# A ConvNeXt block on one core: the first product in pairs of triples, with three PSUM accumulators each

## The chip, the cores and the metric

The kernel runs on one core of a Trainium2 chip. The metric is the device time of one execution, in microseconds; smaller is better. A core has TensorE (PE, its weight loads are PEld), VectorE (DVE), ScalarE (ACT), GpSimd (POOL), and SyncE (SP), which here only issues DMAs.[...] Matmuls write to PSUM[...]; ScalarE and VectorE read it from there[...].

## The reference

A ConvNeXt block is followed by a gate. The input has 32 images of 384 channels and 28 x 28 pixels (784), all in fp32.

```python
# layer 0
y = depthwise_conv7x7(x) + dw_b                  # 384 channels
y = layernorm over channels (ln_g, ln_b)
y = y @ w1 + b1                                  # 384 -> 1536
y = gelu(y)                                      # the exact one
gx = sqrt(sum over pixels of y*y)                # per image and feature
nx = gx / (mean over features of gx + 1e-6)
y = grn_g * (y * nx) + grn_b + y
y = y @ w2 + b2                                  # 1536 -> 384
x = x + y
# layer 1: a gate for each image and channel
avg, mx, mn = mean, max, min of x over the pixels
logits = concat(avg @ W1.T, grouped(mx, W2_1) * W2_2, mn @ W3.T) @ Wfc.T
x = sigmoid(logits[:, :, None, None] + x)
```

## The kernel before

The kernel has two parts. In the first, up to about 496 us, the depthwise convolution of all images is made as matmuls with banded matrices and written to DRAM. GpSimd also makes combined weights there (form_w, L268) and SP stores them to u1d and u2d, one store a step.

The second part goes image by image. For each image, up makes the first product (L559) and down the second (L651). Up of image b+1 stands before down of image b (the loop at L824). Both products use a bilinear scheme: a product of blocks 3 x 3 by 3 x 2 is made with 15 matmuls in place of 18, at the price of additions. The six operand blocks are named 0a to 2b (a and b are the two halves of the pixels), and sums of blocks have the names p to z. They are the "forms": forms_up (L520) makes them for the first product from the normalised image, nine in tiles of their own, and forms (L624) makes them for the second product, each with 128 x 1568 elements.

In up there are KT = 4 triples of three feature blocks each. A triple runs the 15 steps of UPSTEPS (L91). A step has an operand, the weights' sum, a PSUM bank by letter, whether the bank is started anew (1) or added to (0), and what is read from the bank afterwards. "copy" is a copy by ScalarE (L583); "add", "sub", "rsub", "plus" and "minus" are reads by VectorE that combine the bank with what stands in the result y or in a spare tile E (L585 to L593). The banks' values are read in the middle of a sum: bank A, for one, is copied after step x, added to in step v, read again, and so on. A matmul that adds to a bank therefore has to wait until the last reader of that bank is done. A triple uses six banks, A, B, C, D, H and F; D, H and F serve one step each (z, t and 2b). The pool of banks (psz, L416) has seven, in turn for up, down and the transposes of turn. The weights of a triple come in one load of 960 KB, in two buffers (up1, L407).

The result y of a triple then goes through gelu (L549), and square (L553) sums its squares for grn (L602), both on ScalarE. grn makes a scale for each feature. scale (L620) applies it to all 12 blocks of y, on ScalarE for most images, and only then can GpSimd make the forms of the second product. In steady state gelu and square of the triples t-1 and t-2 stand within up; the last gelus, six squares, grn and the scalings stand in the hooks of the down that follows (beside, L735). The same down carries turn (L486) and forms_up for the image after: turn normalises, transposes on TensorE, and ScalarE moves the result out of PSUM.

The program's order is not the order that the engines get. A list scheduler places each instruction by its own estimate of when it can run; so in before it puts the steps z, t and 2b of the first triple of an image ahead of v (banks D, H and F in the trace stand right after A, B and C). In each engine's queue that order is fixed.

Images 0 and 1 start with hooks of their own (start_hooks, L779), since there is no second product yet that could hide their statistics (stats, L458) and transposes.

Of the kernel before, what the change touches and what calls it, by code (L numbers as in the profile page):

```python
# [13 lines left out]
P = 128  # L14
C = 384
# [74 lines left out]

UPSTEPS = (  # L91
# [8 lines left out]
    ("z", "-12", "D", 1, (("D", "add", "2b"),)),  # L100
    ("0b", "-10+11", "A", 0, (("A", "copy", "1b"), ("D", "rsub", "1b"))),
    ("0a", "-00", "B", 0, (("B", "sub", "0a"),)),
    ("t", "+00+10-11", "H", 1, (("H", "add", "E"),)),
    ("q", "-00+01+02-10+11", "A", 0, (("A", "plus", "0b"),)),
    ("u", "+00+10+12", "B", 0, (("B", "minus", "1a"),)),
    ("2b", "-12-20+21+22", "F", 1, (("F", "add", "2b"),)),
)
KT = FB // 3

# [10 lines left out]
def convnext_gate_kernel(  # L120
# [34 lines left out]
    dww = const.tile([P, CB, 49], F32, name="dww")  # L155
    nc.sync.dma_start(dww, dw_w.rearrange("(cb p) t -> p cb t", p=P))
# [8 lines left out]
    awt = const.tile([P, 2, CB, R], F32, name="awt")  # L165
    w22b = const.tile([P, R], F32, name="w22b")
# [8 lines left out]
    with ExitStack() as one:  # L175
# [8 lines left out]
        ws = tp.tile([P, CB * FF], F32, name="ws")  # L184
        tab = tp.tile([P, CB, FL], F32, name="tab")
        dwb = tp.tile([P, C], F32, name="dwb")

# [78 lines left out]
        U1, U2 = 4, 22  # L266

        def form_w(name, wv, text, dst):  # L268

            t = ufp.tile([P, KT, P], F32, tag="uf", name=name)  # L270
            for n, (sg, m, k) in enumerate(terms(text)):
                blk = wv[:, :, int(k), m, :]
                if n == 0:
                    nc.gpsimd.tensor_scalar(t, blk, float(sg), None, ALU.mult)
                else:
                    nc.gpsimd.tensor_tensor(t, t, blk, ALU.add if sg > 0 else ALU.subtract)
            nc.sync.dma_start(dst, t)
# [37 lines left out]
        for s in range(NK):  # L315
# [80 lines left out]
            if si == SK - 1:  # L396
                xt = xn
            i = s - U1
# [8 lines left out]
    up1 = ctx.enter_context(tc.tile_pool(name="up1", bufs=2))  # L407
    up2 = ctx.enter_context(tc.tile_pool(name="up2", bufs=6))
    tep = ctx.enter_context(tc.tile_pool(name="tep", bufs=2))
# [8 lines left out]
    def bank(name):  # L418
        return psz.tile([P, 512], F32, tag="pz", name=name)

    gate = const.tile([P, 3, CB, 3 * R], F32, name="gate")
    nc.vector.memset(gate, 0.0)
    nc.vector.tensor_scalar(gate[:, 0, :, 0:R], awt[:, 0], 1.0 / NT, None, ALU.mult)
    nc.vector.tensor_copy(gate[:, 2, :, 2 * R : 3 * R], awt[:, 1])
    grp = const.tile([P, CB, R], F32, name="grp")
    for cb in range(CB):
        nc.vector.tensor_scalar(grp[:, cb, :], w22b, w21_t[:, cb : cb + 1], None, ALU.mult)

    G = C // R
    grp_a = const.tile([P, CB, R], F32, name="grp_a")
    nc.gpsimd.affine_select(
        out=grp_a, in_=grp, pattern=[[P, CB], [-G, R]], compare_op=ALU.is_ge,
        fill=0.0, base=0, channel_multiplier=1,
    )
    grp_b = const.tile([P, CB, R], F32, name="grp_b")
    nc.gpsimd.affine_select(
        out=grp_b, in_=grp_a, pattern=[[-P, CB], [G, R]], compare_op=ALU.is_ge,
        fill=0.0, base=G - 1, channel_multiplier=-1,  # L440
    )
    nc.vector.tensor_copy(gate[:, 1, :, R : 2 * R], grp_b)
# [102 lines left out]
    def run(hooks, key):  # L545
        for fn in hooks.get(key, ()):
            fn()
# [11 lines left out]
    def up(b, hooks, squares=True):  # L559

        o = feats.pop(b)
        ym = ys[b] = yp.tile([P, FB, NT], F32, tag="y", name=f"y_{b}")
        for t in range(KT):
            wt = up1.tile([P, NS, P], F32, tag="u1", name=f"u1_{b}_{t}")
            nc.sync.dma_start(wt, u1d[t])
            banks = {}
            z = {
                f"{m}{'ab'[h]}": ym[:, 3 * t + m, h * NH : (h + 1) * NH]
                for m in range(3)
                for h in range(2)  # L570
            }
            z["E"] = tep.tile([P, NH], F32, tag="te", name=f"te_{b}_{t}")
            for i, (opnd, _, bk, first, acts) in enumerate(UPSTEPS):
                if first:
                    banks[bk] = bank(f"ph_{b}_{t}_{bk}")
                nc.tensor.matmul(  # L576
                    banks[bk][:, :NH], wt[:, i, :], o[opnd],
                    start=(first == 1), stop=True, skip_group_check=True,
                )
                for src, how, to in acts:  # L580
                    p, d = banks[src][:, :NH], z[to]
                    if how == "copy":
                        nc.scalar.activation(d, p, AF.Identity)  # L583
                    elif how == "add":
                        nc.vector.tensor_tensor(d, d, p, ALU.add)  # L585
                    elif how == "sub":
                        nc.vector.tensor_tensor(d, d, p, ALU.subtract)  # L587
                    elif how == "rsub":
                        nc.vector.tensor_tensor(d, p, d, ALU.subtract)
                    elif how == "plus":  # L590
                        nc.vector.tensor_tensor(d, p, z["E"], ALU.add)  # L591
                    else:
                        nc.vector.tensor_tensor(d, p, z["E"], ALU.subtract)  # L593
                if i in (3, 7, 11):
                    m = (i - 3) // 4
                    if t >= 1:
                        gelu(b, 3 * (t - 1) + m)
                    if t >= 2 and squares:
                        square(b, 3 * (t - 2) + m)
                run(hooks, (t, i))  # L600
# [134 lines left out]
    def beside(b):  # L735
        hooks = {}

        def at(step, fn, *args):
            hooks.setdefault(step, []).append(lambda: fn(*args))

        n = b + 1
        last = n == B - 1
        if n < B:
            for m in range(3):
                at(0, gelu, n, FB - 3 + m)
        if b + 2 < B:
            for j in range(NJ):
                at((0, 0, 1, 1, 2, 2, 3)[j], turn, b + 2, j)
            at(3, forms_up, b + 2)
        if b + 3 < B:  # L750
            at(3, load_y, b + 3)
        if n < B:
            f0 = 0 if b == 0 else FB - 6
            for i in range(f0, FB):
                at((i - f0) // 3 if last else 4 + (i - f0) // (2 if b else 4), square, n, i)
        if b + 3 < B:
            at(8, stats, b + 3)
            at(8, std, b + 3)
        if n < B:
            at(2 if last else 8, grn, n)  # L760
        if b >= 1 and not last:
            at(9, gate_store, b - 1)
        if n < B:
            at(9 if b else 0, load_x, n)
        if n < B:
            for f in range(FB):
                at((2 if last else 10) + f // 3, scale, n, f)
            if last:
                at(6, forms, n, 0, 4)
                at(9, forms, n, 4, EARLY)  # L770
            else:
                at(NS - 1, forms, n, 0, EARLY)
        if b >= 1 and last:
            at(7, gate_store, b - 1)
        return hooks

    def start_hooks():  # L779
        h0, h1 = {}, {}  # L780

        def at(h, t, i, fn, *args):
            h.setdefault((t, i), []).append(lambda: fn(*args))

        V, A = nc.vector, nc.scalar
        if B > 1:
            at(h0, 0, 8, stats, 1)
            at(h0, 0, 8, std, 1)
            for j in range(NJ):
                at(h0, 1, 1 + 2 * j, turn, 1, j, V)  # L790
            at(h0, 1, NS - 1, forms_up, 1)
        if B > 2:
            at(h0, 2, 6, load_y, 2)
        for m in range(3):
            at(h1, 0, 1 + 2 * m, gelu, 0, FB - 3 + m)
        for i in range(6):
            at(h1, i // 5, (8, 10, 11, 12, 13, 0)[i], square, 0, FB - 6 + i)
        if B > 2:
            at(h1, 0, 5, stats, 2)
        at(h1, 1, 1, grn, 0)  # L800
        if B > 2:
            at(h1, 1, 1, std, 2)
        for f in range(FB):
            at(h1, 1 + (6 + f) // 12, (6 + f) % 12, scale, 0, f, A if f % 2 else V)
        at(h1, 2, 8, forms, 0, 0, EARLY)
        return h0, h1

    h0, h1 = start_hooks()
    stats(0)
    std(0)  # L810
    for j in range(NJ):
        turn(0, j, (nc.scalar, nc.vector)[j % 2], (nc.scalar, nc.vector, nc.scalar))
    forms_up(0, nc.vector)
    if B > 1:
        load_y(1)
    up(0, h0)
    load_x(0)
    if B > 1:
        up(1, h1, squares=False)
    else:  # L820
        for fs in h1.values():
            for fn in fs:
                fn()
    for b in range(B):  # L824
        if b >= 1 and b + 1 < B:
            up(b + 1, {})
        down(b, beside(b))
# [40 lines left out]
```

## Time and profile before

| | us |
|---|---|
| median of three runs (3218.94 to 3219.2) | 3219.02 |
| the profiled execution, its time | 3216.78 |
| the profiled execution, its span | 3215.1 |
| depthwise part, to the last matmul of it | about 496 |
| first product, image 10 | 40.33 |
| second product, image 9, with its transposes | 43.86 |

| ScalarE, one instruction | mean ns | count |
|---|---|---|
| scale, 784 columns (L484) | 1027 | 378 |
| gelu (L551) | 941 | 384 |
| square (L557), and its accumulator read | 851 and 189 | 384 each |
| copy of a bank in up (L583) | 483 to 496 | 640 |
| table load | 1283 | 97 |

VectorE's reads of a bank in up take 558 to 567 ns, a form of the second product on GpSimd 3512 to 3518, one of the first 1020.

How to read it: the times of the page are sums over the profiled execution. A row of a group has the busy time, the mean of one instruction, and the idle time of the engine just before, with what ended it. In the rows of the order in time, the columns are start and length in us, the engine and line, the operation, and how many instructions stand in the row. One fp32 matmul appears as two passes, each with its weight load, and a pass of 392 columns lasts longer (492 ns) than the distance to the next (329 ns), since they are pipelined.

### The profile page before, as it was taken

To read this page: it belongs to the slowest core of one execution; us is meant where nothing else is said; L and a number is where in the kernel's file an instruction comes from. 1 tells how busy PE (TensorE), PEld (TensorE's weight loads), DVE (VectorE), ACT (ScalarE), POOL (GpSimd) and SP (SyncE) were. 2 spreads that over 40 slices of the span, in tenths; PEclk is the share of its full clock that TensorE was granted. 3 is DMA by queue.
4 is the path that set the end of the run, shared out by engine and by line. 5 is a ranking of instruction groups with operands and counts; after the bars stand their busy time and mean duration, and the time that the engine had idled before them with its cause. 6 is when DMAs were issued, how large, how long until landed. Compare 5 with 4: busy or idle time off the path is not lost.

```text
span 3215.1 us, 35678 instructions
## 1 busy us (share of the span) xinstructions
PE 3174.8 (99%) x12352; PEld 2009.1 (62%) x12352; DVE 1669.3 (52%) x3442; ACT 1886.1 (59%) x3032; POOL 1607.1 (50%) x821
## 2 busy tenths in 40 slices
PE   8999998999999999999999999999999999999998
PEld 7999995555555555555555555555555555555555
DVE  3443436555555555555555555555555555555553
ACT  2222225766666666666666666666666666666662
POOL 2453511645555555555555555555555555555554
PEclk9999999999999999999999999999999999999999
DMA  9999985444444444344444444444444444444333
GB/s 346 364 340 359 341 296 183 131 131 136 130 139 143 141 141 139 132 136 143 134 142 145 134 145 143 136 140 139 146 146 129 137 129 141 142 141 141 125 101 126
DMA packets 257160, 540.84 MB, mean 168 GB/s; under 512 B 121021, under 2 KB 130774, under 8 KB 247766
## 3 DMA queue, kind: packets, MB, share of 16 engines
q1 hardware_dynamic: 244148, 500.70, 46.1%
q10 hardware_dynamic: 12834, 37.88, 3.5%
q8 instruction: 98, 1.61, 0.2%
q14 instruction: 80, 0.66, 0.1%
HBM read 447.53 MB, written 90.99 MB: 167 GB/s over the span
## 4 chain that ended last, share of the span: by engine, by line
PE 98%; DVE 1%; ACT 1%; DMA 1%; issue 0%; SPq 0%; ACTq 0%; POOL 0%; DVEq 0%; POOLq 0%
PE ph_A L576 14%; PE ph_B L576 13%; PE pz_A L673 11%; PE pz_B L673 10%; PE pz_C L673 5%; PE pz_E L673 5%; PE ph_C L576 5%; PE pc L344 5%; PE pc L345 4%; PE pc L348 4%; PE pz_F L673 3%; PE ph_D L576 3%; PE ph_H L576 3%; PE ph_F L576 3%; PE pz_G L673 3%; PE pz_D L673 3%
## 5 line engine op out<-in xcount | busy, mean ns | idle before, releaser
L648 POOL TENSOR_TENSOR d_v<-d_u,y 128x1568 f32<-128x1568 f32 x32 | 112.4, 3512 | 759.4 <-PE pz_B L673 735.4
L551 ACT ACTIVATE y<-y,fv 128x784 f32<-128x784 f32 x384 | 346.7, 941 | 214.5 <-DVE y L591 213.8
L484 ACT ACTIVATE y<-y,fv,gsc 128x784 f32<-128x784 f32 x378 | 358.6, 1027 | 30.1 <-DVE gsc L618 30.1
L557 ACT ACTIVATE junk<-y 128x784 f32<-128x784 f32 x384 | 326.7, 851 | 5.0
L648 POOL TENSOR_TENSOR d_p<-y 128x1568 f32<-128x1568 f32 x31 | 109.1, 3518 | 434.7 <-ACT y L484 434.7
L576 PE MATMUL ph_A<-af,u 128*128 128x392 f32 x768 | 313.7, 502 | 5.5 <-DVE af L542 5.4
L362 ACT ACTIVATE yc<-pc,dwb 128x224 f32<-128x224 f32 x192 | 103.8, 641 | 367.1 <-PE pc L348 264.4
L576 PE MATMUL ph_B<-af,u 128*128 128x392 f32 x768 | 311.3, 493 | 0.3 <-ACT y L583 0.3
L673 PE MATMUL pz_A<-y,u 128*128 128x392 f32 x768 | 268.8, 493 | 0.0
L648 POOL TENSOR_TENSOR y<-d_v,y 128x1568 f32<-128x1568 f32 x64 | 223.4, 3514 | 2.5
L576 PEld LDWEIGHTS ph_A<-af,u 128*128 128x128 f32 x768 | 136.4, 190 | 135.3 <-ACT y L583 57.8
L576 PE MATMUL ph_A<-acc,u 128*128 128x392 f32 x512 | 216.4, 504 | 0.0
L344 PE MATMUL pc<-xt,tmat 128*128 128x224 f32 x768 | 209.4, 354 | 6.7 <-issue 4.9
L576 PE MATMUL ph_B<-acc,u 128*128 128x392 f32 x512 | 213.6, 499 | 0.1
L576 PEld LDWEIGHTS ph_B<-af,u 128*128 128x128 f32 x768 | 145.2, 190 | 109.0 <-DVE y L587 9.6
L673 PEld LDWEIGHTS pz_A<-y,u 128*128 128x128 f32 x768 | 145.8, 190 | 106.4
L583 ACT ACTIVATE y<-ph_A 128x392 f32<-128x392 f32 x256 | 124.7, 487 | 145.0 <-PE ph_A L576 144.9
L237 POOL COPY xpad<-xi 128x784 f32<-128x784 f32 x96 | 80.6, 841 | 254.4 <-PE pt L248 188.1
L587 DVE TENSOR_TENSOR y<-y,ph_A 128x392 f32<-128x392 f32 x128 | 72.0, 563 | 238.9 <-PE ph_A L576 228.1
L473 ACT ACTIVATE sd<-mv,eps_t 128x7 f32<-128x7 f32 x32 | 9.6, 300 | 314.3 <-DVE mv L468 314.3
L542 POOL TENSOR_TENSOR af<-af,acc 128x392 f32<-128x392 f32 x186 | 187.2, 1020 | 4.9
L348 PE MATMUL pc<-xt,tmat 128*128 128x192 f32 x768 | 187.6, 326 | 0.0
(160 smaller groups left out, 7007.1 us busy)
## 6 DMA issues: line engine op xcount, KB each, us to landing
u<-u1d SPq DMA_DIRECT2D x128, 960.0 KB, 4.7
u<-u2d SPq DMA_DIRECT2D x480, 256.0 KB, 2.7
tmat<-fs SPq DMA_DIRECT2D x48, 1420.0 KB, 9.3
yd<-yc SPq DMA_DIRECT2D x22, 1792.0 KB, 8.4
yi<-yd SPq DMA_DIRECT2D x32, 1232.0 KB, 6.8
xi<-in_x SPq DMA_DIRECT2D x96, 392.0 KB, 9.4
x<-in_x SPq DMA_DIRECT2D x32, 1176.0 KB, 5.8
out<-x ACTq DMA_DIRECT2D x31, 1176.0 KB, 5.0
```

What stands on the lines that cost most here:

```text
L344: nc.tensor.matmul(pc[:, ci, :N], t[:, c, P : 2 * P], xc, start=True, stop=False)
L345: nc.tensor.matmul(pc[:REACH, ci, : N - B], t[:, c, 2 * P : T0 + MW], xc[:, B:], start=False, stop=False)
L348: nc.tensor.matmul(pc[:, ci, B:N], t[:, c, :P], xc[:, : N - B], start=False, stop=True)
L362: nc.scalar.activation(yc[:, :, :, cy + ci].rearrange("p b j -> p j b"), pc[:, ci, :N].rearrange("p (j b) -> p j b", j=NJ), AF.Identity, b ...
L484: eng.activation(out, in_, AF.Identity, bias=add, scale=mul)
L542: eng.tensor_tensor(d, o[in0], o[in1], op)
L551: nc.scalar.activation(y, y, AF.Gelu, bias=b1_t[:, f : f + 1], scale=1.0)
L557: nc.scalar.activation(junk, ys[b][:, f, :], AF.Square, accum_out=ssqs[b][:, f : f + 1])
L576: nc.tensor.matmul(banks[bk][:, :NH], wt[:, i, :], o[opnd], start=(first == 1), stop=True, skip_group_check=True,)
L583: nc.scalar.activation(d, p, AF.Identity)
L648: nc.gpsimd.tensor_tensor(d, o[in0], o[in1], op)
L673: nc.tensor.matmul(pz[:, :NH], wt[:, t, :], o[opnd][:, t, :], start=(first == 1 and t == 0), stop=(t == KT - 1), skip_group_check=True,)
```

## The change

The first product takes two triples together: each step is done for triple t2 and then for t2+1. Each triple has only the banks A, B and C; z, t and 2b start C anew. Weights come in thirds of five steps, in six buffers of the size of a third. Gelu and square leave the loop of up. Their places are given by hooks for each image (within, beside): in the steady state six gelus and three squares in the second pair of up, the others in down, and the 12 scalings of the image before in the first pair of up, with the blocks that the form p reads put first. grn is one step later. Image 1 starts in another way too.

```diff
-    ("z", "-12", "D", 1, (("D", "add", "2b"),)),
-    ("0b", "-10+11", "A", 0, (("A", "copy", "1b"), ("D", "rsub", "1b"))),
+    ("z", "-12", "C", 1, (("C", "add", "2b"),)),
+    ("0b", "-10+11", "A", 0, (("A", "copy", "1b"), ("C", "rsub", "1b"))),
...
-    ("t", "+00+10-11", "H", 1, (("H", "add", "E"),)),
+    ("t", "+00+10-11", "C", 1, (("C", "add", "E"),)),
...
-    ("2b", "-12-20+21+22", "F", 1, (("F", "add", "2b"),)),
+    ("2b", "-12-20+21+22", "C", 1, (("C", "add", "2b"),)),
...
+UG = 5
...
-    up1 = ctx.enter_context(tc.tile_pool(name="up1", bufs=2))
+    up1 = ctx.enter_context(tc.tile_pool(name="up1", bufs=6))
...
-    tep = ctx.enter_context(tc.tile_pool(name="tep", bufs=2))
+    tep = ctx.enter_context(tc.tile_pool(name="tep", bufs=3))
...
-        for t in range(KT):
-            wt = up1.tile([P, NS, P], F32, tag="u1", name=f"u1_{b}_{t}")
-            nc.sync.dma_start(wt, u1d[t])
...
-                if i in (3, 7, 11):
-                    m = (i - 3) // 4
-                    if t >= 1:
-                        gelu(b, 3 * (t - 1) + m)
-                    if t >= 2 and squares:
-                        square(b, 3 * (t - 2) + m)
-                run(hooks, (t, i))
+        for t2 in range(0, KT, 2):
             for i, (opnd, _, bk, first, acts) in enumerate(UPSTEPS):
+                for t in (t2, t2 + 1):
+                    if i % UG == 0:
+                        wts[t] = up1.tile([P, UG, P], F32, tag="u1", name=f"u1_{b}_{t}_{i}")
+                        nc.sync.dma_start(wts[t], u1d[t, :, i : i + UG, :])
...
+                    if first and i < 3:
+                        banks[t, bk] = bank(f"ph_{b}_{t}_{bk}")
...
+                    run(hooks, (t2, 2 * i + t - t2))
```

The hooks of up in the new kernel (V is VectorE, A is ScalarE, HF = 6; a key is the pair's first triple and the matmul in the pair):

```python
order = [f for f in range(FB) if f % 3] + [f for f in range(FB) if f % 3 == 0]

def squared(b):
    return 0 if b == 1 else HF if b in (0, B - 1) else HF // 2

def within(b):
    hooks, at = adder()
    p = b - 1
    if b == 0:
        if B > 1:
            at((0, 12), stats, 1)
            at((0, 12), std, 1)
            for j in range(NJ):
                at((0, 18 + 2 * (j // 2)), turn, 1, j, V)
            at((0, 24), forms_up, 1)
...
    elif b == 1:
        for m in range(HF):
            at((0, 2 + 2 * m), gelu, p, HF + m)
            at((0, 16 + 2 * m), square, p, HF + m)
...
        at((0, 29), grn, p)
...
        for i, f in enumerate(order):
            at((2, 1 + i), scale, p, f, V if i % 3 else A)
        at((2, 12), forms, p, 0, EARLY)
    else:
        for i, f in enumerate(order):
            at((0, 2 * i), scale, p, f)
        at((0, 24), forms, p, 0, EARLY)
    if b != 1:
        for m in range(HF):
            at((2, 2 + 4 * m), gelu, b, m)
        for m in range(squared(b)):
            at((2, 28 if m >= HF // 2 else 22 + 2 * m), square, b, m)
    return hooks
```

In beside, the remaining gelus stand in steps 0 and 1 of the second product, the remaining squares from step 3 on (step 1 for the last image), grn in step 9 (4), gate_store in step 10 (9). The scalings stand there only for the last image.

Three smaller edits go with it. form_w no longer issues its store; a list holds it, and it is issued at the next step of the depthwise part. The gate's weights are made in a function called at step 40 of that part in place of after it, and the second affine_select writes to gate directly. The tiles dww, awt, w22b, grp and grp_a are in the pool that is released after the depthwise part.

More of the change, by code (lines that the diff above doesn't have):

```diff
@@ L152, in convnext_gate_kernel @@
     yl = dram.tile([P, NLAST, B, NJ * YC], F32, name="yl")
-    dww = const.tile([P, CB, 49], F32, name="dww")
-    nc.sync.dma_start(dww, dw_w.rearrange("(cb p) t -> p cb t", p=P))
     ident = const.tile([P, P], F32, name="ident")
@@ L164, in convnext_gate_kernel @@
     nc.gpsimd.memset(ones_f, 1.0 / FF)
-    awt = const.tile([P, 2, CB, R], F32, name="awt")
-    w22b = const.tile([P, R], F32, name="w22b")
+    gate = const.tile([P, 3, CB, 3 * R], F32, name="gate")
     wfc = const.tile([3 * R, C], F32, name="wfc")
@@ L184, in convnext_gate_kernel @@
         ws = tp.tile([P, CB * FF], F32, name="ws")
+        dww = tp.tile([P, CB, 49], F32, name="dww")
+        nc.sync.dma_start(dww, dw_w.rearrange("(cb p) t -> p cb t", p=P))
         tab = tp.tile([P, CB, FL], F32, name="tab")
         dwb = tp.tile([P, C], F32, name="dwb")
+        awt = tp.tile([P, 2, CB, R], F32, name="awt")
+        w22b = tp.tile([P, R], F32, name="w22b")
+        grp = tp.tile([P, CB, R], F32, name="grp")
+        grp_a = tp.tile([P, CB, R], F32, name="grp_a")
         NT2 = 4
@@ L266, in convnext_gate_kernel, with gate_weights @@
         U1, U2 = 4, 22
+        stores = []
+        SG = 40
+        def gate_weights():
+            nc.vector.memset(gate, 0.0)
+            nc.vector.tensor_scalar(gate[:, 0, :, 0:R], awt[:, 0], 1.0 / NT, None, ALU.mult)
+            nc.vector.tensor_copy(gate[:, 2, :, 2 * R : 3 * R], awt[:, 1])
+            for cb in range(CB):
+                nc.vector.tensor_scalar(
+                    grp[:, cb, :], w22b, w21_t[:, cb : cb + 1], None, ALU.mult
+                )
+            G = C // R
+            nc.gpsimd.affine_select(
+                out=grp_a, in_=grp, pattern=[[P, CB], [-G, R]], compare_op=ALU.is_ge,
+                fill=0.0, base=0, channel_multiplier=1,
+            )
+            nc.gpsimd.affine_select(
+                out=gate[:, 1, :, R : 2 * R], in_=grp_a, pattern=[[-P, CB], [G, R]],
+                compare_op=ALU.is_ge, fill=0.0, base=G - 1, channel_multiplier=-1,
+            )
         def form_w(name, wv, text, dst):
@@ L276, in form_w @@
                     nc.gpsimd.tensor_tensor(t, t, blk, ALU.add if sg > 0 else ALU.subtract)
-            nc.sync.dma_start(dst, t)
+            stores.append((dst, t))
         AHEAD = 6
@@ L397, in convnext_gate_kernel @@
                 xt = xn
+            if s == SG:
+                gate_weights()
+            for dst, u in stores:
+                nc.sync.dma_start(dst, u)
+            stores.clear()
             i = s - U1
@@ L419, in bank @@
         return psz.tile([P, 512], F32, tag="pz", name=name)
[L423 to L442, printed above, removed]
     x_tiles, yts, sts, accs, pts, feats = {}, {}, {}, {}, {}, {}
@@ L557, in square, with up @@
         nc.scalar.activation(junk, ys[b][:, f, :], AF.Square, accum_out=ssqs[b][:, f : f + 1])
-    def up(b, hooks, squares=True):
+    def up(b, hooks):
         o = feats.pop(b)
         ym = ys[b] = yp.tile([P, FB, NT], F32, tag="y", name=f"y_{b}")
-        for t in range(KT):
-            wt = up1.tile([P, NS, P], F32, tag="u1", name=f"u1_{b}_{t}")
-            nc.sync.dma_start(wt, u1d[t])
[L566 to L572, printed above, removed]
-            for i, (opnd, _, bk, first, acts) in enumerate(UPSTEPS):
[L574 to L593, printed above, removed]
-                if i in (3, 7, 11):
-                    m = (i - 3) // 4
-                    if t >= 1:
-                        gelu(b, 3 * (t - 1) + m)
-                    if t >= 2 and squares:
-                        square(b, 3 * (t - 2) + m)
-                run(hooks, (t, i))
@@ new lines, in up @@
+        wts, banks, zs = {}, {}, {}
+        for t2 in range(0, KT, 2):
+            for i, (opnd, _, bk, first, acts) in enumerate(UPSTEPS):
+                for t in (t2, t2 + 1):
+                    if i % UG == 0:
+                        wts[t] = up1.tile([P, UG, P], F32, tag="u1", name=f"u1_{b}_{t}_{i}")
+                        nc.sync.dma_start(wts[t], u1d[t, :, i : i + UG, :])
+                    if i == 0:
+                        zs[t] = {
+                            f"{m}{'ab'[h]}": ym[:, 3 * t + m, h * NH : (h + 1) * NH]
+                            for m in range(3)
+                            for h in range(2)
+                        }
+                        zs[t]["E"] = tep.tile([P, NH], F32, tag="te", name=f"te_{b}_{t}")
+                    z = zs[t]
+                    if first and i < 3:
+                        banks[t, bk] = bank(f"ph_{b}_{t}_{bk}")
+                    nc.tensor.matmul(
+                        banks[t, bk][:, :NH], wts[t][:, i % UG, :], o[opnd],
+                        start=(first == 1), stop=True, skip_group_check=True,
+                    )
+                    for src, how, to in acts:
+                        p, d = banks[t, src][:, :NH], z[to]
+                        if how == "copy":
+                            nc.scalar.activation(d, p, AF.Identity)
+                        elif how == "add":
+                            nc.vector.tensor_tensor(d, d, p, ALU.add)
+                        elif how == "sub":
+                            nc.vector.tensor_tensor(d, d, p, ALU.subtract)
+                        elif how == "rsub":
+                            nc.vector.tensor_tensor(d, p, d, ALU.subtract)
+                        elif how == "plus":
+                            nc.vector.tensor_tensor(d, p, z["E"], ALU.add)
+                        else:
+                            nc.vector.tensor_tensor(d, p, z["E"], ALU.subtract)
+                    run(hooks, (t2, 2 * i + t - t2))
@@ L729, in gate_store, with adder @@
             nc.scalar.dma_start(ov, xt)
-    def beside(b):
+    HF = FB // 2
+    V, A = nc.vector, nc.scalar
+    order = [f for f in range(FB) if f % 3] + [f for f in range(FB) if f % 3 == 0]
+    def adder():
         hooks = {}
@@ L739, in at, with beside @@
             hooks.setdefault(step, []).append(lambda: fn(*args))
+        return hooks, at
+    def squared(b):
[3 more added lines that the diff above has]
+        p = b - 1
+        if b == 0:
+            if B > 1:
+                at((0, 12), stats, 1)
+                at((0, 12), std, 1)
+                for j in range(NJ):
+                    at((0, 18 + 2 * (j // 2)), turn, 1, j, V)
+                at((0, 24), forms_up, 1)
+            if B > 2:
+                at((2, 0), load_y, 2)
+        elif b == 1:
+            for m in range(HF):
+                at((0, 2 + 2 * m), gelu, p, HF + m)
+                at((0, 16 + 2 * m), square, p, HF + m)
+            if B > 2:
+                at((0, 8), stats, 2)
+            at((0, 29), grn, p)
+            if B > 2:
+                at((0, 29), std, 2)
+            for i, f in enumerate(order):
+                at((2, 1 + i), scale, p, f, V if i % 3 else A)
+            at((2, 12), forms, p, 0, EARLY)
+        else:
+            for i, f in enumerate(order):
[6 more added lines that the diff above has]
+                at((2, 28 if m >= HF // 2 else 22 + 2 * m), square, b, m)
+        return hooks
+    def beside(b):
+        hooks, at = adder()
         n = b + 1
         last = n == B - 1
-        if n < B:
-            for m in range(3):
-                at(0, gelu, n, FB - 3 + m)
         if b + 2 < B:
@@ L752, in beside @@
         if n < B:
-            f0 = 0 if b == 0 else FB - 6
-            for i in range(f0, FB):
-                at((i - f0) // 3 if last else 4 + (i - f0) // (2 if b else 4), square, n, i)
+            g0 = 0 if n == 1 else HF
+            for f in range(g0, FB):
+                at((f - g0) // 3, gelu, n, f)
+            s0 = squared(n)
+            for f in range(s0, FB):
+                at((1 if last else 3) + (f - s0) // 2, square, n, f)
         if b + 3 < B:
             at(8, stats, b + 3)
-            at(8, std, b + 3)
+            at(9, std, b + 3)
@@ L759, in beside @@
         if n < B:
-            at(2 if last else 8, grn, n)
+            at(4 if last else 9, grn, n)
         if b >= 1 and not last:
-            at(9, gate_store, b - 1)
+            at(10, gate_store, b - 1)
         if n < B:
[L764 to L772, printed above, removed]
@@ L773, in beside @@
-        if b >= 1 and last:
-            at(7, gate_store, b - 1)
-        return hooks
[L779 to L806, printed above, removed]
@@ L808, in convnext_gate_kernel @@
-    h0, h1 = start_hooks()
+            at(10 if b else 0, load_x, n)
+        if last:
+            for i, f in enumerate(order):
+                at(4 + i // 3, scale, n, f)
+            at(8, forms, n, 0, 4)
+            at(9, forms, n, 4, EARLY)
+            if b >= 1:
+                at(9, gate_store, b - 1)
+        return hooks
     stats(0)
@@ L811, in convnext_gate_kernel @@
     for j in range(NJ):
-        turn(0, j, (nc.scalar, nc.vector)[j % 2], (nc.scalar, nc.vector, nc.scalar))
-    forms_up(0, nc.vector)
+        turn(0, j, (A, V)[j % 2], (A, V, A))
+    forms_up(0, V)
     if B > 1:
         load_y(1)
-    up(0, h0)
+    up(0, within(0))
     load_x(0)
     if B > 1:
[L819 to L823, printed above, removed]
+        up(1, within(1))
     for b in range(B):
         if b >= 1 and b + 1 < B:
-            up(b + 1, {})
+            up(b + 1, within(b + 1))
         down(b, beside(b))
```

## The prediction

> **What bounds the kernel now.** I read the page's busy times and chain first, then the groups by form, what the weight loads waited for, and the order in time of one image.
>
> ```profile
> PE 3174.8 (99%) x12352; PEld 2009.1 (62%) x12352; DVE 1669.3 (52%) x3442; ACT 1886.1 (59%) x3032; POOL 1607.1 (50%) x821
> ...
> PE 98%; DVE 1%; ACT 1%; DMA 1%; issue 0%; SPq 0%; ACTq 0%; POOL 0%; DVEq 0%; POOLq 0%
> ```
>
> TensorE is busy throughout and is 98% of the chain; every other engine is idle 40% or more. No work of TensorE's is removed, so only the little time in which it issues below its pace can be won. The groups by form show where that is: one matmul is two passes (two records), and a pass of 392 columns that is not held up lasts 492 or 493 ns.
>
> ```profile
> L576 PE MATMUL ph_A<-af,u 128*128 128x392 f32 x768 | 313.7, 502 | 5.5 <-DVE af L542 5.4
> L576 PE MATMUL ph_B<-acc,u 128*128 128x392 f32 x512 | 213.6, 499 | 0.1
> L673 PE MATMUL pz_A<-y,u 128*128 128x392 f32 x768 | 268.8, 493 | 0.0
> ```
>
> The first product (L576) has groups above it, most of the second (L673) has not. What its weight loads waited for, from 545 us on:
>
> ```profile
> PEld ph_A L576 <- ACT y L583: 56.3, 122, 0.8
> PEld ph_A L576 <- ACT te L583: 49.3, 118, 0.6
> PEld ph_B L576 <- DVE te L589: 25.7, 89, 0.4
> PEld ph_B L576 <- DVE y L587: 24.6, 62, 0.8
> ```
>
> An accumulator that is added to again waits until ScalarE has copied, or VectorE has read, its last value. These waits come to 155.9 us, but a weight load stands one pass (0.33 us) ahead of its matmul, so most of that is cover. What reaches the matmuls is read from the order in time, image 10 of 32 here (rows of PE, PEld and ACT from three such answers):
>
> ```profile
> 1143.83 0.82 PE L576 MATMUL ph_A<-af,u 128*128 128x392 f32 x2
> 1144.49 0.82 PE L576 MATMUL ph_B<-af,u 128*128 128x392 f32 x2
> ...
> 1164.02 0.82 PE L576 MATMUL ph_A<-af,u 128*128 128x392 f32 x2
> ...
> 1173.90 0.82 PE L576 MATMUL ph_A<-af,u 128*128 128x392 f32 x2
> ...
> 1184.16 2.80 PE L673 MATMUL pz_G<-y,u 128*128 128x392 f32 x8
> ```
> ```profile
> 1151.08 0.30 PEld L576 LDWEIGHTS ph_B<-acc,u 128*128 128x128 f32 x2 [0.48 <-DVE y L587]
> 1151.82 0.30 PEld L576 LDWEIGHTS ph_A<-acc,u 128*128 128x128 f32 x2 [0.44 <-ACT te L583]
> ```
> ```profile
> 1144.69 0.50 ACT L583 ACTIVATE y<-ph_A 128x392 f32<-128x392 f32 x1 [1.09 <-PE ph_A L576]
> ```
>
> The third triple (1164.02 to 1173.90) has no stall: 15 matmuls in 9.88 us, 0.6587 each. The whole first product took 1184.16 - 1143.83 = 40.33 us; 60 x 0.6587 = 39.52. So 0.81 us an image is lost to late accumulators, 25.1 us over the 31 images after the first. That is all the first product has to give. A copy starts 0.20 us after the next matmul began (1144.69 against 1144.49); I use that as the latency.
>
> **What the Trainium skill says.** "Trainium Perfetto Trace Analysis", Identifying the Most-Contended Engine: a busy matmul row is no measure of how near TensorE is to its best, look at weight loads too. The trace agrees: 99% busy, and yet passes of 597 ns among those of 492. The same page, Matmuls: independent groups should rotate through different PSUM banks, so that evacuation lies beside the next group's matmuls. Two triples side by side do that, fewer banks for each undo part of it. "TensorE: Matmul & The Clock Gate", Architectural detail: the queue can pull a weight load ahead of a running matmul; here it does, by one pass. "ScalarE: Activation LUTs", What ACT_TABLE_LOAD costs: a load of 1283 ns, and activations that follow each other overlap by 93 ns. The trace has 1283 ns and an overlap of 94.
>
> **The change part by part.** I count in matmuls from the start of the first product, T = 0.659 k at the start of the k-th; its result is free for a copy at 0.659 (k + 1) + 0.20, and a matmul that waits must be let go by 0.659 k - 0.33.
>
> *Two triples side by side.* An accumulator that came back three steps, 1.98 us, later in the written order comes back six matmuls, 3.95 us, later. From the end of a matmul the copy takes 0.20 + 0.49 = 0.69; the limit is 5 x 0.659 - 0.33 = 2.96 us after that end. ScalarE may thus be 2.2 us late, more than two of its longest operations (1.03). Before, it could be late by 0.3. The waits listed above go: -25.1 us.
>
> *Three accumulators.* C is used for s and 2a, then restarted for z, for t and for 2b. z and 2b wait only for VectorE's last read three steps back, which is wide. t is narrow: it may not restart C before VectorE has subtracted z from the copy that ScalarE makes of 0b, two steps earlier. For the first triple of a pair: 0b is k = 18, copy from 12.72 to 13.21, VectorE 0.06 + 0.56 to 13.83; t is k = 22, let go by 14.17. Spare: 0.34 us. So what ScalarE has ahead of that copy decides. In the changed program's order of instructions, the first pair has six of the twelve scalings behind it, done in the second product before, and six left: ten copies of 0.39 and six scalings of 0.93 (with the overlap) make 9.5 us, all queued before 0b's copy at 12.72. No stall. The second pair has a table load, three gelus that wait for the results of step 2b of the first pair (k = 28, VectorE done at 19.9), then copies and three more gelus to about 25.8, three squares of 0.98 (with the accumulator read) to 28.7, then E's copies and three squares between and after them to 32.4. 0b's copy is due at 0.659 x 49 + 0.20 = 32.5. It just fits, with 0.34 in reserve. I take 0.1 us an image, 3 us; the bounds are 0 and 0.4 (one square's half behind), 12 us. A gain is excluded, as the wait is new.
>
> *ScalarE's division.* Gelus, squares and scalings change places; their number doesn't. In the first product it will be busy some 20 copies 9.8 + 6 scalings 6.2 + 6 gelus 5.6 + 6 squares 6.2 + a table load 1.3 = 29.1 us of 39.5, against 26.4 of 40.3 now. Three table loads an image stay three. The scalings end about 10 us into the first product, so the forms on GpSimd start at about 5 us in place of 0: seven of 3.52 end at about 30, before the second product begins at 39.5, and its fourth step, which first needs more than p, comes later still. d_v waits for a buffer in any case (25.25 us of it now). Cost 0; it would need some 9 us more delay to show.
>
> *Weights in thirds.* Twelve loads of 320 KB an image for four of 960. Each waits for a buffer freed six loads earlier, that is for a matmul 20 or more before the one that needs it, 13 us; the large ones land in 4.8. Behind them on SP stand the second product's later weights, which wait for buffers that free after that. Cost 0; exposed it would be under 3 us an image.
>
> *Gate weights, stores deferred, tiles moved.* The gate's instructions already ran at 2 to 131 us, beside the depthwise product; they still do. The weight forms' stores go one step later on SP, out of the way of input loads; TensorE's stalls in that part are at most 2 us that this could touch. I take 0, bounds -2 and +1.
>
> *The start, 504 to 590 us.* Before the first triples VectorE makes the forms, to 510.8; now its next instructions are the seven statistics of image 1 (0.46 apart), which wait for a transfer that was issued at 504.8 and landed 6.5 later. They end at 514.6, before VectorE has a product to read (516.6). TensorE's second matmul is now A again, and waits for A's copy: 0.9 us. Image 1's transposes in the first product wait for banks, some tenths each, and in image 1 squares and a table load precede 0b's copy, 0.65. Together I take +1, bounds -3 and +6.
>
> Sum: -25.1 + 3 + 0 + 1 = -21. The profiled execution is 3216.78 us (its span 3215.1); 3196 for its like. The runs' median is 2.24 above it, so 3198.
>
> **The rivals.**
> - *A, as above:* 3198, from 3191 to 3205. For it: the waits are named, and six matmuls cover two ScalarE operations. Chance 0.62.
> - *B, half of it comes back* through t and the order the scheduler chose: every second pair is late by 0.5 to 0.6 us through ScalarE's squares, 31 x 0.4 = 12, so 3207. For it: the second pair's spare is only 0.34. Chance 0.16.
> - *C, no change:* the scheduler hoists z, t and 2b of a triple to the front now (D, H, F at 1145.80 to 1147.12) and can't with a shared C. If that was what hid VectorE's reductions at the start of the stage (to 1146.5), the 0.81 stays: 3218. Against: VectorE's first read now comes at k = 6, 4.8 us, after they are done. Chance 0.09.
> - *D, slower:* t becomes the stage's bound. Place: 0b's copy behind one more scaling or gelu (0.93) in each pair. Price: 0.93 - 0.34 = 0.6 a pair, 1.2 an image, 37 us; less 25, +12: 3231. It decides from 0.41 us a pair on, that is, ScalarE 0.75 us later than I have it. For it: ScalarE is strictly in order, and its work in the stage rises by 2.7 us. Chance 0.13.
>
> **How the numbers follow.** Predicted is A's 3198. The range reaches from A's best, 3190, over B to just short of C, 3214. About 0.2% (6.4 us) is what a measurement here tells from no change. Faster by more: A and B, 0.78; within: C, 0.09; slower: D, 0.13.
>
> **What would show it.** Weight-load waits on the first product's accumulators fall from 155.9 us to a few tens, and its passes to 493 ns in all groups; the first product takes 39.5 to 39.7 us an image, the second 43.9 as now. Wrong would be: weight loads of ph_C that wait for VectorE's subtraction from 0b (then B or D); d_s or d_t among the second product's waits (ScalarE's scalings come too late); or a stretch from 504 to 600 us that is longer by over 6.

## The result and the profile after

The changed kernel takes 3207.27 us (median of 6 runs, 3206.84 to 3207.99) against 3218.91 (6 runs) for the one before: ratio 0.9966, 95% interval 0.9956 to 0.9976. That is 11.6 us less; 21 were forecast. Its profiled execution has a span of 3205.3 us, against 3215.1.

The page of the changed kernel: busy times, the shares of the chain, and the three groups that were shown of before.

```profile
PE 3157.5 (99%) x12352; PEld 2035.2 (63%) x12352; DVE 1660.7 (52%) x3443; ACT 1874.7 (58%) x3028; POOL 1607.1 (50%) x821
...
PE 87%; ACT 11%; issue 1%; DVE 1%; DMA 1%; SPq 0%; ACTq 0%; POOL 0%; DVEq 0%; POOLq 0%
...
L592 PE MATMUL ph_A<-af,u 128*128 128x392 f32 x768 | 287.0, 496 | 5.9 <-DVE af L552 5.3
...
L683 PE MATMUL pz_A<-y,u 128*128 128x392 f32 x768 | 268.5, 492 | 0.0
...
L592 PE MATMUL ph_B<-acc,u 128*128 128x392 f32 x512 | 189.5, 492 | 0.0
```

A pass of the two groups of the first product took 499 and 502 ns before and takes 492 now (the mean of 496 for ph_A comes from six passes of 861 to 1022 ns in the first 5 us of the first image). So that loss is gone. But the chain, 98% TensorE before, now runs for 11% through ScalarE, although TensorE is as busy as before: somewhere TensorE must be released by ScalarE again and again. The waits of the changed kernel (sum, how many, longest) say where:

```profile
PEld py L512 <- ACT yn L494: 20.2, 31, 4.6
PE py L512 <- ACT yn L494: 12.6, 31, 4.3
...
PEld ph_A L592 <- ACT y L599: 2.2, 2, 1.8
PEld ph_C L592 <- DVE y L605: 1.6, 5, 0.6
```

The 155.9 us on the first product's accumulators are down to 3.8 in these two lines. New are the transposes of `turn`, for the image after next: TensorE itself waits 31 times for ScalarE's normalised piece `yn`. (`turn` handles an image in seven pieces, yn_0 to yn_6; each piece has a triple of transposes.) In the kernel before the same lines read:

```profile
PEld py L502 <- ACT yn L484: 13.2, 32, 4.6
PE py L502 <- ACT yn L484: 4.6, 2, 4.3
```

There the weight loads waited 32 times, too, but the matmuls only twice, both at the start. The order in time shows what lay between. The kernel before, from the start of the second product at 1184.16 (counted from 0 that of image 7, and the first product ahead of it that of image 8, where the text above says 9 and 10; rows of PE and ACT; columns are start, length, engine, line, operation, count, and in brackets the idle time ahead with its releaser); d_s is the form s of the second product, read in its fourth step:

```profile
1184.16 2.80 PE L673 MATMUL pz_G<-y,u 128*128 128x392 f32 x8
...
1193.37 0.49 PE L502 MATMUL py<-ident,yn 128*128 128x128 f32 x3
...
1193.38 1.30 ACT L484 ACTIVATE yn<-yi,nmr,rstd 128x384 f32<-128x384 f32 x2
...
1193.70 0.82 PE L673 MATMUL pz_E<-d_s,u 128*128 128x392 f32 x2
...
1194.36 0.49 PE L502 MATMUL py<-ident,yn 128*128 128x128 f32 x3
```

The changed kernel, one whole round:

```profile
1226.24 1.48 PE L592 MATMUL ph_A<-af,u 128*128 128x392 f32 x4
...
1265.74 2.80 PE L683 MATMUL pz_G<-y,u 128*128 128x392 f32 x8
...
1274.95 0.49 PE L512 MATMUL py<-ident,yn 128*128 128x128 f32 x3
...
1274.96 1.30 ACT L494 ACTIVATE yn<-yi,nmr,rstd 128x384 f32<-128x384 f32 x2
...
1275.72 0.55 PE L512 MATMUL py<-ident,yn 128*128 128x128 f32 x3 [0.28 <-ACT yn L494]
...
1276.11 2.80 PE L683 MATMUL pz_E<-d_s,u 128*128 128x392 f32 x8
...
1310.10 1.48 PE L592 MATMUL ph_A<-af,u 128*128 128x392 f32 x4
```

Set both against the start of their second product. The fifth triple of transposes comes 9.21 us after it in both, and ScalarE starts the sixth piece 9.22 us after it in both (1193.38 - 1184.16, 1274.96 - 1265.74). ScalarE is exactly as late as it was. But before, the scheduler had put one d_s matmul (two passes) between the fifth triple and the sixth; now all six transposes stand together and all of the d_s matmuls behind them. What covered the wait has moved. TensorE took none of the d_s matmuls ahead of the transposes that waited: the first starts at 1276.11.

The stages of one image, from such starts (median over the images; "later" is the version of the first experiment below):

| us | before | changed | later |
|---|---|---|---|
| first product | 40.32 | 39.50 | 39.50 |
| second product | 43.87 | 44.36 | 43.87 |
| start of the first product | 510.3 | 511.9 | 512.2 |

The first products of all images come to 1296.24 us before and 1270.26 after, -26.0; the second products of the first 30 images to 1314.51 and 1328.53, +14.0; the start to +1.6. With +0.6 for the last two images' second products and the end, that is the -9.8 by which the span fell.

The wait of 0.28 us in brackets is less than the 0.49 that an image loses: it is counted from the modelled end of the pass before. From start to start, the sixth triple comes 0.77 us after the fifth (1275.72 - 1274.95), where three transposes take 0.33 when nothing holds them: 0.44 late. The row itself lasts 0.55 in place of 0.49, and with that the image's loss is accounted for.

### The profile page after: what moved, and what is told of

The parts are those of the page before. It is cut to its first block, busy times and chain, and to the rows that moved or that the text cites. A ratio compares the mean times of both kernels' runs of the same rounds, so it can differ in the third digit from the quotient of the medians.

```text
span 3205.3 us, 36222 instructions
## 1 busy us (share of the span) xinstructions
PE 3157.5 (99%) x12352; PEld 2035.2 (63%) x12352; DVE 1660.7 (52%) x3443; ACT 1874.7 (58%) x3028; POOL 1607.1 (50%) x821
## 4 chain that ended last, share of the span: by engine, by line
PE 87%; ACT 11%; issue 1%; DVE 1%; DMA 1%; SPq 0%; ACTq 0%; POOL 0%; DVEq 0%; POOLq 0%
PE ph_A L592 13%; PE ph_C L592 12%; PE ph_B L592 12%; PE pz_A L683 11%; PE pz_B L683 8%; PE pz_E L683 5%; PE pz_C L683 5%; ACT y L561 5%; PE pc L372 5%; PE pc L373 4%; PE pc L376 4%; PE pz_F L683 3%; ACT junk L567 3%; PE pt L253 2%; ACT acc L494 2%; ACT yn L494 2%
## 5 line engine op out<-in xcount | busy, mean ns | idle before, releaser
L494 ACT ACTIVATE y<-y,fv,gsc 128x784 f32<-128x784 f32 x376 | 366.8, 1041 | 100.2 <-DVE gsc L628 100.2
L592 PE MATMUL ph_A<-af,u 128*128 128x392 f32 x768 | 287.0, 496 | 5.9 <-DVE af L552 5.3
L592 PE MATMUL ph_B<-af,u 128*128 128x392 f32 x768 | 284.4, 492 | 0.0
L592 PE MATMUL ph_C<-af,u 128*128 128x392 f32 x768 | 284.3, 492 | 0.0
L601 DVE TENSOR_TENSOR y<-y,ph_C 128x392 f32<-128x392 f32 x384 | 215.8, 562 | 31.9 <-PE ph_C L592 1.0
L592 PEld LDWEIGHTS ph_A<-af,u 128*128 128x128 f32 x768 | 146.3, 191 | 114.0 <-DVE af L552 5.7
L592 PEld LDWEIGHTS ph_C<-af,u 128*128 128x128 f32 x768 | 145.7, 190 | 107.4 <-DVE y L605 1.6
L592 PE MATMUL ph_A<-acc,u 128*128 128x392 f32 x512 | 189.6, 492 | 0.0
L592 PE MATMUL ph_C<-acc,u 128*128 128x392 f32 x512 | 189.6, 492 | 0.0
L592 PE MATMUL ph_B<-acc,u 128*128 128x392 f32 x512 | 189.5, 492 | 0.0
```

Source lines behind the costliest of these rows:

```text
L494: eng.activation(out, in_, AF.Identity, bias=add, scale=mul)
L592: nc.tensor.matmul(banks[t, bk][:, :NH], wts[t][:, i % UG, :], o[opnd], start=(first == 1), stop=True, skip_group_check=True,)
```

## The experiments

Theory 1: the missing half is the wait for `yn_5`, because no matmul stands in front of it any more. Theory 2, its rival: that wait is cover for another, and taking it away brings little. Theories 3 and 4: the new division of ScalarE's work caused the loss, or was needed for the gain. In what follows a ratio is to the kernel before, with its 95% interval in brackets.

**The sixth transposes one step later.** In `beside`, of the changed kernel:

```diff
-                at((0, 0, 1, 1, 2, 2, 3)[j], turn, b + 2, j)
+                at((0, 0, 1, 1, 2, 3, 3)[j], turn, b + 2, j)
```

> The changed kernel with one figure altered: the sixth normalisation and its three transposes are called one step later in the second product, so that TensorE's queue has the four d_s matmuls (4 x 0.66 us) between the fifth triple of transposes and the sixth; ScalarE's queue is the same. Theory 1 (what is missing of the forecast gain is TensorE's wait for ScalarE's yn_5, 0.50 us in each of 30 images more than before, because no matmul stands in front of those transposes any more): that wait goes, the excess of the transposes falls from 23 us to under 8, and the time from 3207.3 to 3190-3194 us. Rival theory 2 (the wait covers another one: what follows in the second product would be late anyway): under 5 us of gain, 3203-3208, and another wait of about 0.5 us an image appears in the second product.

Measured: 3192.43 us (3192.25 to 3192.54), ratio 0.992 (0.9907 to 0.9934). Its chain and its waits:

```profile
PE 98%; DMA 1%; DVE 0%; issue 0%; ACT 0%; POOL 0%; SPq 0%; ACTq 0%; DVEq 0%; POOLq 0%
```
```profile
PEld py L512 <- ACT yn L494: 5.3, 2, 4.6
PE py L512 <- ACT yn L494: 4.6, 2, 4.3
```

14.8 us faster than the changed kernel; the 31 waits are down to the two of the start, and ScalarE has left the chain. No other wait came in their place: the second product is back at 43.87. Theory 2 falls.

**The sixth piece by VectorE.** The other end of the wait, with TensorE's order as in the changed kernel:

```diff
-                at((0, 0, 1, 1, 2, 2, 3)[j], turn, b + 2, j)
+                at((0, 0, 1, 1, 2, 2, 3)[j], turn, b + 2, j, V if j == 5 else A)
```

> The changed kernel with the sixth normalisation (yn_5) done by VectorE in place of ScalarE; TensorE's queue is that of the changed kernel, six transposes together. It is the other end of the same wait: yn_5 no longer stands behind three squares and three evacuations in ScalarE's queue. Theory 1: same gain as with the transposes put later, 3190-3195 us, and the waits for yn under L494 fall to a few us. Theory 2 (cover for another wait): 3203-3208. If VectorE's extra 0.4-0.6 us an image delayed the additions that free the accumulators of the second product, the gain would be given back as waits for VectorE: 3205-3212.

Measured: 3192.96 us, ratio 0.9921 (0.9907 to 0.9934). The groups by form show the 30 pieces on VectorE (40 with the start's ten), 489 ns on average:

```profile
L492 DVE TENSOR_SCALAR yn<-yi,rstd,nmr 128x384 f32<-128x384 f32 x40 | 19.4, 489 | 2.4 <-PE py L512 1.4 <-ACT yn L494 0.8
```

The second product is again 43.87 us. So it was this one piece in ScalarE's queue, and either end of the wait can be mended, for the same gain. VectorE, idle for half of the span, gave nothing back.

**The control: the same step in the kernel before.**

> The kernel before with the same one-figure edit, as a control. There one d_s matmul (0.66 us) already stood between the two triples of transposes, and the transposes' excess is only 7.8 us in the whole run. Theory 1: a gain of at most 8 us, 3211-3219. If it gains as much as the changed kernel does with the same edit, the wait was in the kernel before too and theory 1 doesn't explain the difference between forecast and result. Theory 2: no change, 3217-3220.

Measured: 3217.74 us, ratio 0.9998 (0.999 to 1.0007): nothing. Its second product stays at 43.87. The one d_s matmul had covered the wait in full; the wait of the matmuls is the changed kernel's own.

**The scalings back beside the second product.** In `within`, the twelve `scale` and the first `forms` are taken out of the branch of the later images, and put into `beside`:

```diff
+        if n < B and not last:
+            for i, f in enumerate(order):
+                at(10 + i // 3, scale, n, f)
+            at(NS - 1, forms, n, 0, EARLY)
```

> The changed kernel with the twelve scalings and the first four forms put back beside the second product, as before; ScalarE's queue around yn_5 stays that of the changed kernel. Theory 1 and the prediction (where ScalarE's scalings stand costs nothing, the paired product and the squares decide): 3205-3210. Rival theory 3 (ScalarE's new division as a whole caused the lost half, through the scalings that now stand beside the first product): 10-15 us faster, 3192-3197. Rival theory 4 (the scalings had to leave the second product for the gain to come): 3212-3225.

Measured: 3206.9 us, ratio 0.9966 (0.9953 to 0.9978), the changed kernel's time; stages 39.50 and 44.36. In the traces the edit moves less than the text of the program: of the twelve scalings the changed kernel does six beside the first product (the scheduler had put the other six beside the second already), this version one, the kernel before none. For these five the place makes neither the gain nor the loss, and theories 3 and 4 fall as far as they go. The squares and gelus were not moved alone; what they do is not shown.

**The three banks alone.** The kernel before, with `UPSTEPS` of the changed one:

```diff
-    ("t", "+00+10-11", "H", 1, (("H", "add", "E"),)),
+    ("t", "+00+10-11", "C", 1, (("C", "add", "E"),)),
```

(and C for D in z and 0b, C for F in 2b.)

> The kernel before with the three-accumulator assignment alone: triples one after another, as before. From the start of 0b to the earliest start of t on the freed bank is about 2.1 us in the changed kernel's trace, and unpaired there are only two passes (1.32 us) between: 0.8-1.0 us in 124 triples less what the late accumulators of before absorb: +80 to +120 us, 3300-3340. Theory: three banks are what the pairing has to pay for and no gain in themselves. Rival: fewer accumulators free the pool and bring part of the gain without the pairing: under 3219.

Measured: 3244.56 us, ratio 1.0082 (1.0068 to 1.0096), 26.5 us slower: the sign of the theory, less than a third of its size. The waits:

```profile
PEld ph_C L576 <- DVE y L589: 37.9, 96, 0.4
PEld ph_C L576 <- ACT y L583: 32.4, 62, 0.7
PEld ph_A L576 <- DMA u<-u1d: 26.5, 30, 2.1
...
PE ph_A L576 <- DMA u<-u1d: 6.8, 22, 1.5
```

The estimate had the written order, with two matmuls' distance from 0b to t. In the program's order on TensorE, q or a matmul of the next triple stands ahead of t, so the waits on C are 0.4 and 0.5 us on average, not 0.9. And a new wait came: with triples mixed by the scheduler and two buffers of whole weights, the matmuls wait 6.8 us for transfers, which the changed kernel's thirds do not show at all.

This run tells one thing more, from its order in time:

```profile
1202.12 1.19 PE L502 MATMUL py<-ident,yn 128*128 128x128 f32 x6
...
1202.75 0.31 PEld L502 LDWEIGHTS py<-ident,yn 128*128 128x128 f32 x3 [0.39 <-ACT yn L484]
```

The six transposes stand together here too, and take 1.19 us for 0.82: 0.37 in each of 30 images, 11 of the 26.5 us. Counted from start to start against the usual 0.329 us, in the images after the first two, the passes on C come 14 us late in all and those that waited for a transfer 12, while what the kernel before loses on A and B falls from 24 to 9. So the three banks alone bring no gain, but that they lose by themselves is not shown: what is late on C is about what is won on A and B, and the loss stands with the transposes and the transfers. ScalarE's division is the old one and nothing is paired. It is enough to change the banks, then, for the order that hid the wait to be given up. Why it does so was not followed into the scheduler.

**The smaller edits alone.** The kernel before, with the gate weights, the deferred stores and the tile moves.

> The kernel before with only the smaller edits: the gate weights built in the convolution, the stores of the formed weights a step later, tiles moved between pools. The prediction put them at 0 (-2 to +1) and the start at +1 (-3 to +6): 3216-3222. Rival: they bring part of the result's 11.6 us: 3208-3214.

Measured: 3218.46 us, ratio 1.0001 (0.9992 to 1.0009). They are worth nothing, as forecast. The first product starts at 511.7 here, at 510.3 before: of the order of what the runs differ by there (510.3 to 512.8 over all of them).

**How much spare the restart of t has.** To the version with later transposes, reads of the same 392 columns by ScalarE are added ahead of 0b's copy; nothing of the result depends on them:

```diff
+                    if i == 9 and t == t2:
+                        extra = junkp.tile([P, NT], F32, tag="junk", name=f"extra_{b}_{t}")
+                        nc.scalar.activation(extra[:, :NH], banks[t, "A"][:, :NH], AF.Identity)
```

> The version with the transposes one step later (3192.4 us), and before the copy of 0b in the first triple of each pair one more ScalarE read of the same 392 columns (nothing of the computation changes). In the changed kernel's trace the copy of 0b starts at 1238.95, the subtraction that frees bank C ends at 1240.04 and the weights of t load about 1240.39: spare about 0.35 us; back-to-back copies start 0.377 us apart. Theory (the restart of t has 0.34 us of spare, as the prediction took): the extra 0.377 us is used up to within 0.04 us, 62 pairs, +0 to +5 us: 3192-3197. Rival (the restart has no spare, so a delay goes straight through): 62 x 0.377 = +23 us, 3215.

Measured: 3202.49 us, 10.1 above the version without it, and no wait explains that image by image: its first product is 39.50 us in every later image. All of it lies in the first two images' first products (85.39 to 95.43 us), where the trace has 2.7 us of TensorE's wait for VectorE's addition from C and 4.7 for its subtraction into E, around 590 us. ScalarE's second copy of E, on which the latter waits, comes there only at 589.35. It is the order of that early stretch which has changed with the added instruction, and it wasn't followed further. One later pair, in the order in time:

```profile
1412.70 0.50 ACT L598 ACTIVATE extra<-ph_A 128x392 f32<-128x392 f32 x1 [2.79 <-PE ph_A L592]
1413.10 0.88 ACT L602 ACTIVATE y<-ph_A 128x392 f32<-128x392 f32 x2
...
1414.24 1.09 PEld L592 LDWEIGHTS ph_C<-af,u 128*128 128x128 f32 x4 [0.23 <-DVE y L608]
1414.48 1.48 PE L592 MATMUL ph_C<-af,u 128*128 128x392 f32 x4
```

The copy is 0.40 us later, the weight load of t waits 0.23 (without a delay it is 0.14, as a load of 0.19 follows every 0.33), and the pass loses nothing. With a second read:

> As the run before, with two extra reads. Theory of 0.34 us spare: 0.754 - 0.35 = 0.40 us in each of 62 pairs, +25 us: 3212-3222, and waits of ph_C for VectorE's y of about 25 us in the trace. No spare: +47 us, 3239. Spare of a whole pass (0.66 us, counted to the pass instead of to its weight load): +6 us, 3198.

Measured: 3219.09 us. Its later images take 40.02 us in the first product, 0.52 more, 0.26 a pair:

```profile
1415.78 0.50 ACT L598 ACTIVATE extra<-ph_A 128x392 f32<-128x392 f32 x1 [2.79 <-PE ph_A L592]
...
1416.55 0.89 ACT L603 ACTIVATE y<-ph_A 128x392 f32<-128x392 f32 x2
...
1417.71 0.30 PEld L592 LDWEIGHTS ph_C<-af,u 128*128 128x128 f32 x2 [0.62 <-DVE y L609]
1417.71 1.58 PE L592 MATMUL ph_C<-af,u 128*128 128x392 f32 x4
```

The copy is 0.77 us late and costs 0.26. A delay of 0.40 is thus within the spare and one of 0.77 is not; if every further part of a delay costs its own length, which was not measured between the two, the spare is 0.51 us: between the 0.35 counted to the weight load's usual place and the 0.66 counted to the pass. The totals, 25 us expected and 26.7 found, agree by luck: some 10 of it again lies in the first two images (95.04 us), which the expectation did not have, and a pair costs 0.26 where it had 0.40.

## Why the prediction was half right

Taken in its own steps:

- *Two triples side by side, -25.1.* Right: the first product went from 40.32 to 39.50 us where 39.52 was the floor, -26.0 over all images and 25.1 of it in the 30 after the first two. Its waits vanish as said.
- *Three accumulators, +3 for t.* A little too dear: 1.6 us of weight-load waits in the whole run and none that shows in a stage. The spare is over 0.40 us, by the doses about 0.5, where 0.34 was taken.
- *ScalarE's division, 0, and with it the second product.* This is the step that failed. It followed ScalarE's queue through the first product and GpSimd's forms into the second, and then let the second product stand at "43.9 as now". It is 44.36. What it left out is not on ScalarE at all: the five scalings that were moved back had no effect, and ScalarE is as late as before (9.22 us after the stage's start). What changed is TensorE's own order in the second product. A wait of the weight loads, 32 times, could be read in the kernel before; it was covered by one matmul, and the order of the changed program, which was read for the first product, had that matmul behind the transposes. The price is 0.49 us an image, 14.0 in all, and with it the sum becomes -26.0 + 14.0 + 1.6 + 0.6 for the end, the -9.8 of the spans.
- *Weights in thirds, gate, stores and moves, 0; the start, +1.* Right: no wait of the first product for a transfer, and 3218.46 for the small edits alone. The +1.6 at the start agrees, but says little, as the start differs by 2.5 us among the runs.

Of the rivals, B gave 3207 and 3207 came, but by chance: it had t late through ScalarE's squares, and t isn't late. The range took in 3207 for B's sake, so the measured time lies within it for a reason that did not hold. C's worry about VectorE's reductions and D's about t as the bound did not come about; by the doses, D's price begins beyond 0.40 us of delay, not at 0.34.

The predicted 3198 would have been too cautious for the mechanism and too bold for the kernel: with the sixth transposes one step later the same change gives 3192.4.

## What to carry to other kernels

A wait that costs nothing is still a wait: list the late arrivals that something covers, with the instruction that covers each, and look in the changed order of every stage whether it still stands there, also in stages that the edit doesn't name. An engine that is busy 99% before and after can hide half a microsecond a round; the share of another engine in the chain (ScalarE here: 1% before, 11% after) shows it at once. And after such a change try the cheap remedy from both ends of the new wait: here one call a step later was worth 14.8 us, more than the 11.6 of the change itself.

## What the runs showed of the hardware

A matmul is not late as soon as its weight load is. The load of t normally stands 0.33 us ahead of its pass; delayed to 0.24 us ahead (the first dose) it cost the pass nothing. With the second dose load and pass start together in the trace (1417.71 both); the pass came 0.15 us late and the next one another 0.10, the same in each of the 56 pairs of images 3 to 30. So weight-load waits overstate what is lost: 14.6 us of them on ph_C with one extra read stand for no loss in any later image.

Two copies of 392 columns on ScalarE that follow each other start 0.38 to 0.40 us apart though each lasts 0.50; a copy in front of another therefore delays it by less than its own length.
